# V2 on four column tiles, W1 behind W2, W0 on another queue: the start of a feature-interaction kernel, reordered

## The chip, the cores and the metric

The kernel runs on one core of one Trainium2 chip. The metric is device time in microseconds, the median over runs; less is better. The core has a matmul engine (TensorE, PE in the profile, its weight loads listed apart as PEld), a vector engine (DVE), a scalar engine (ACT), GpSimd (POOL) and SyncE (SP). PE writes to PSUM banks alone; DVE and ACT copy from there. ACT, POOL and SP each issue DMA transfers from a queue of their own; the 16 DMA engines of the core carry them all.

## The reference

`x` is 1024 x 39 x 64 (batch, field, embedding). Three layers of the same form follow one another; their sums over the embedding are weighted by `fc_w` and added.

```python
def _cin_layer(Xk, X0, W, b):
    O = W.shape[0]
    Hk, Fdim = (Xk.shape[1], X0.shape[1])
    Wr = W.reshape(O, Hk, Fdim)
    return jnp.einsum('bhe,bfe,ohf->boe', Xk, X0, Wr) + b[None, :, None]
X0 = sparse_embedding
Xk = X0
outs = []
for W, b in ((W0, b0), (W1, b1), (W2, b2)):
    Xk = _cin_layer(Xk, X0, W, b)
    outs.append(Xk.sum(axis=-1))
cin_output = jnp.concatenate(outs, axis=-1)
return cin_output @ fc_w.T + fc_b
```

W0 is 64 x 1521 (39 x 39 pairs of fields), W1 and W2 are 64 x 2496 (64 x 39). All is float32.

## The kernel before

**What it computes with.** The last two layers only feed one number per sample, so the kernel folds their weights: W2 and `fc_w` give `v2`, a 64 x 40 table (V2; its last column is the second third of `fc_w`); W1 and `v2` give T, for each pair of fields a column of 64. W0 turned and T lie side by side in `both`: W0's part in partitions 0 to 63, T's in 64 to 127. A symmetric pair of fields is then one row of weights (`pairs`), turned by PE into `wa`. The main work is a product of two fields' values for each pair (DVE, `product`, L210), multiplied on PE by `wa` into `po` (`multiply`, L502).

**Blocks.** The batch is 32 blocks of 32 samples (2048 columns). Each block has six chunks of 128 pairs; two blocks share a chunk of pairs left over (`join`, L522 and L533). The operands of the products are gathers: rows of a table in device memory (`xd`, three tables for two blocks each, every one with two rows of ones) picked by index lists that DVE computes at the start (`lists`, L313 to L374). `gather_rows` (L170) runs on POOL. For block 0 the tiles 0 to 3 are gathered in two halves from `xh`, two half blocks that are loaded straight from `x` (L244); tile 4 and everything later comes from `xd`, and `xd[0]` is copied from `xh` by SyncE (L383).

**The order of the start.** Every engine does its instructions in the order in which the program lists them.

- SyncE's queue: `fcrow` (L240), the first half `xh[0]` (L244), and later the two copies `xd[0]` from `xh` (L383).
- ACT's queue: W2 (L241), W0 in two parts (L250), W1 in two halves (L255), `xh[1]` (L244); then a first copy that brings in ACT's table (L259).
- POOL: constants, then the rows of ones for the three tables (L344), the biases and `fc_b` (L348 to L351, five small transfers), then the gathers: tiles 0 to 3 of the first half, the load of block 1, tiles 0 to 3 of the second half, tile 4 and so on.
- DVE: the lists, with the identity `unit` (L318) and `fc2` (L319) among them. `fc2` holds the last third of `fc_w`, twice, in two columns of zeros: column 0 for even rows, column 32 for odd rows, since W2 lies in 128 partitions, two for each output.
- PE: filler matmuls (`spin`, L271) whose results nobody reads; the `fcrow2` matmul that turns a row of `fc_w` (L310); fillers; V2's four matmuls (L393) into two banks `pv`; four more turned rows of `fc_w` (`turn_row`, L354); 20 transposes of W0 (L407) into two banks `pw`; then T's 39 matmuls (L439) into four banks, of which the last two are `pv`; three fillers; the first turn of `pairs` (L486), one filler, the first products (L502). A float32 matmul shows as two passes in the profile, a transpose as one.
- Between them DVE turns V2 by two block transposes (L413) and DVE and ACT copy it into `v2` (L418 to L420); both copy W0 (L435) and T (L450) into `both`, then build `pairs` (L466 to L470).

Transfers signal semaphores. Those of SP's and ACT's queues go round eight semaphores, POOL's round eight others; one that takes a semaphore again waits for the landing of the earlier transfer that has it.

Of the kernel before, what the change touches and what calls it, by code (L numbers as in the profile page):

```python
# [54 lines left out]
F32 = mybir.dt.float32  # L55
I32 = mybir.dt.int32
AF = mybir.ActivationFunctionType
ALU = mybir.AluOpType
# [3 lines left out]
FH = F * H  # L62
FT = F + 1
# [80 lines left out]
def cin_kernel(ctx: ExitStack, tc: tile.TileContext, x, w0t, b0, w1, b1, w2, b2, fc_w, fc_b, out):  # L144
# [71 lines left out]
    with prep as prep:  # L216
# [5 lines left out]
        fc2 = prep.tile([128, H], F32, name="fc2")  # L222
# [20 lines left out]
        def load_half(k, engine):  # L243
            engine.dma_start(  # L244
                xh[k].rearrange("f (b e) -> b f e", e=E), x[k * SB : (k + 1) * SB]
            )

        load_half(0, nc.sync)
        for s, n in enumerate((NW, F - NW)):
            nc.scalar.dma_start(  # L250
                w0s[H * s : H * s + F, 0 : n * H], w0v[:, s * NW * H : (s * NW + n) * H]
            )
        for s in range(2):
            part = slice(s * FH // 2, (s + 1) * FH // 2)
            nc.scalar.dma_start(w1s[:, part], w1[:, part])  # L255
# [6 lines left out]
        pv = [bank("pv") for _ in range(2)]  # L262
        pt = [bank("pt") for _ in range(2)] + pv
# [48 lines left out]
        )  # L312
        nc.vector.tensor_copy(row, place)  # L313
# [4 lines left out]
        nc.vector.tensor_scalar(unit, apart, 0, None, ALU.is_equal)  # L318
        nc.vector.tensor_scalar(fc2[:, 0::32], mask, small[:, 0:1], None, ALU.mult)  # L319
# [14 lines left out]
        nc.vector.tensor_scalar(lists[:, NT : 2 * NT], fields_of, float(FT), None, ALU.add)  # L334

# [7 lines left out]
        for k in range(NTAB):  # L343
            nc.gpsimd.dma_start(xd[k][F::FT].rearrange("r (p c) -> p r c", c=128), ones)  # L344


        for k, t in enumerate((b1, b2)):
            nc.gpsimd.dma_start(bias[:, k : k + 1], t.rearrange("(h o) -> h o", o=1))  # L348
        for h in (0, H):
            nc.gpsimd.dma_start(b0s[h : h + H], b0.rearrange("(h o) -> h o", o=1))  # L350
        nc.gpsimd.dma_start(fcb, fc_b.rearrange("(p o) -> p o", o=1))  # L351

        def turn_row(dst, k):
            nc.tensor.matmul(dst, fcrow[:, k * H : k * H + H], one, start=True, stop=True)  # L354

        spin(2)
# [31 lines left out]
        blocks = prep.tile([128, 2, 320], F32, name="blocks")  # L388
        w2v = w2s.rearrange("p (h f) -> p h f", f=F)
        for k in range(2):  # L390
            for u in range(2):
                f0 = u * 19 + k * 10
                nc.tensor.matmul(  # L393
                    pv[k][H * u : H * u + H, 0:320],
                    fc2,
                    w2v[:, :, f0 : f0 + 10],
                    start=True,
                    stop=True,
                )

        for k in range(3):
            turn_row(small[0:H, k + 1 : k + 2], k)
        turn_row(small[H:128, 4:5], 0)
        for s in range(2):
            for k in range(NW // 2):
                n = min(128, (F - NW * s) * H - k * 128)
                nc.tensor.transpose(  # L407
                    pw[s][0:n, k * FT : k * FT + F],
                    w0s[H * s : H * s + F, k * 128 : k * 128 + n],
                    unit[H * s : H * s + F, H * s : H * s + F],  # L410
                )
        for k in range(2):
            nc.vector.transpose(  # L413
                blocks[:, k].rearrange("p (f h) -> p f h", h=32),
                pv[k][:, 0:320].rearrange("p (h f) -> p f h", f=10),
            )
        column = blocks.rearrange("h k (f j) -> h (k f) j", j=32)[:, :, 0]
        nc.scalar.copy(v2[:, F:FT], small[0:H, 2:3])  # L418
        nc.vector.tensor_copy(v2[:, 0:20], column[0:H])
        nc.scalar.copy(v2[:, 20:F], column[H:128, 1:20])  # L420
# [8 lines left out]
        copies = (nc.vector.tensor_copy, nc.scalar.copy)  # L429

        for k, (a, n) in enumerate(((0, NW), (NW, F - NW))):
            for t in range(2):
                m = (n + 1 - t) // 2
                src = pw[k][H * t : H * t + H, 0 : m * FT].rearrange("h (a b) -> h a b", b=FT)
                copies[k](bothv[0:H, a + t : a + t + 2 * m - 1 : 2, 0:F], src[:, :, 0:F])  # L435
        w1v = w1s.rearrange("o (h f) -> o f h", f=F)
        for a in range(F):
            q, g, t = a // (2 * NQ), a // 2 % NQ, a % 2
            nc.tensor.matmul(  # L439
                pt[q][H * t : H * t + H, g * FT : g * FT + FT],  # L440
                w1v[:, a],
                v2,
                start=True,
                stop=True,
            )
        for q in range(4):
            for t in range(2):
                a = 2 * NQ * q + t
                m = len(range(a, min(F, 2 * NQ * (q + 1)), 2))
                copies[t](  # L450
                    bothv[H:128, a : a + 2 * m - 1 : 2],
                    pt[q][H * t : H * t + H, 0 : m * FT].rearrange("h (a b) -> h a b", b=FT),
                )
        spin(3)
# [268 lines left out]
```

## Time and profile before

| what | us |
|---|---|
| median of four runs | 741.48 |
| the four runs | 739.51 to 744.95 |
| the profiled execution | 738.22 |
| its span, first to last instruction | 736.4 |
| PE busy | 727.6 (99%) |
| DVE busy | 638.2 (87%) |
| ACT busy | 165.0 (22%) |
| POOL busy | 388.6 (53%) |
| V2's matmuls, from | 5.89 |
| W0's transposes, from | 7.63 |
| T's matmuls, from | 11.09 |
| first gather, from | 11.67 |
| first product matmul (L502), from | 21.54 |

All places are counted from the span's start. Busy shares are means over the whole span, so they hide the start, which lasts some 20 us of 736. A line of a timeline gives start, length, engine, line, operation, out<-in, the count, and in brackets the idle time before it with what ended it. "Issue" is time in which an engine waited for nothing that the profile shows.

### The profile page before, as it was taken

The page shows a single profiled execution, that of the slowest core. Times are in us where ns is not written, and L with a number is a line of the kernel's source. Part 1 is how long each engine was busy: PE and PEld are TensorE (multiplying, and loading weights), DVE is VectorE, ACT ScalarE, POOL GpSimd, SP SyncE. Part 2 cuts the span into 40 slices and gives each one's busy share as a digit, 9 for nine tenths or more (in the row PEclk, how much of TensorE's full clock was granted, in tenths as well). Part 3 has the DMA queues.
Part 4 walks back from the last instruction along what each step waited for, and adds up shares of the span by engine and source line. Part 5 has one row for each costly group of instructions (what it writes and reads, how often), then busy time and mean ns, then how long its engine had stood idle before and what let it go on. Part 6 is the DMA issues. An engine that isn't in the chain of part 4 may idle for free.

```text
span 736.4 us, 6511 instructions
## 1 busy us (share of the span) xinstructions
PE 727.6 (99%) x2456; PEld 319.6 (43%) x2456; DVE 638.2 (87%) x516; ACT 165.0 (22%) x238; POOL 388.6 (53%) x256
## 2 busy tenths in 40 slices
PE   7999999999999999999999999999999999999998
PEld 5444444444444444444444444444444444444443
DVE  4899999888899888899888899888899888899885
ACT  2232122221212222122221212222122221212222
POOL 6848864457545365554457545365554457545300
PEclk8899999999999999999999999999999999999999
DMA  7889997877676796757877676795767876566700
GB/s 201 296 334 354 337 394 296 335 283 273 239 277 253 291 347 237 270 238 276 330 277 277 238 278 255 288 356 220 267 251 271 335 284 252 213 259 247 285 1 1
DMA packets 63656, 197.25 MB, mean 268 GB/s; under 512 B 37684, under 2 KB 37733, under 8 KB 43656
## 3 DMA queue, kind: packets, MB, share of 16 engines
q0 software_dynamic: 29040, 186.22, 65.5%
q1 hardware_dynamic: 33534, 8.79, 5.2%
q10 hardware_dynamic: 1050, 1.83, 1.0%
q8 instruction: 19, 0.31, 0.2%
q14 instruction: 13, 0.11, 0.0%
HBM read 196.76 MB, written 10.60 MB: 282 GB/s over the span
## 4 chain that ended last, share of the span: by engine, by line
PE 97%; DMA 1%; DVE 1%; ACTq 0%; issue 0%; ACT 0%
PE po L502 90%; PE po L522 4%; PE po L533 2%; DMA w1s<-in_w 1%; PE idle L271 1%; PE pv L439 0%; PE pt L439 0%; DVE p L210 0%; PE tr L486 0%; ACTq L250 0%; DVE g L552 0%; DVE sums L574 0%; ACT z L550 0%; ACTq L255 0%; ACTq L241 0%
## 5 line engine op out<-in xcount | busy, mean ns | idle before, releaser
L502 PE MATMUL po<-p,wa 128*128 128x512 f32 x1536 | 665.2, 593 | 0.6 <-DVE p L210 0.6
L210 DVE TENSOR_TENSOR p<-r 128x2048 f32<-128x2048 f32 (+2 forms) x198 | 434.3, 2225 | 74.4 <-PE po L502 71.0
L170 POOL DMA_INDIRECT r<-xd,lists x156 | 307.6, 1972 | 282.9 <-issue 269.3
L502 PEld LDWEIGHTS po<-p,wa 128*128 128x128 f32 x1536 | 290.2, 190 | 371.3 <-issue 351.5
L550 ACT ACTIVATE z<-po,fc0s 64x512 f32<-64x512 f32 x128 | 87.4, 683 | 381.5 <-PE po L533 218.6
L552 DVE SCALAR_TENSOR_TENSOR g<-po,b0s,z 64x512 f32<-64x512 f32 x128 | 95.9, 749 | 9.3 <-ACT z L550 5.3
L545 ACT COPY g<-r 39x1024 f32<-39x1024 f32 x64 | 66.7, 1043 | 155.5 <-DVE sums L563 122.1
L563 DVE TENSOR_REDUCE sums<-g 103x16 f32<-103x1024 f32 x62 | 75.6, 1220 | 2.1
L170 POOL DMA_INDIRECT v<-xd,lists x16 | 29.3, 1829 | 4.9 <-issue 4.9
L170 POOL DMA_INDIRECT u<-xd,lists x16 | 29.1, 1819 | 4.9 <-issue 4.9
L522 PE MATMUL po<-p,wa 32*64 32x512 f32 x512 | 31.6, 600 | 0.0
L212 DVE TENSOR_TENSOR p<-u,v 128x1024 f32<-128x1024 f32 x16 | 19.5, 1217 | 0.0
L522 PEld LDWEIGHTS po<-p,wa 32*64 32x64 f32 x512 | 9.4, 131 | 20.2 <-issue 20.2
L533 PE MATMUL po<-u,wa 32*64 32x512 f32 x256 | 17.0, 587 | 0.0
L170 POOL DMA_INDIRECT r<-xh,lists x8 | 10.5, 1317 | 6.1 <-issue 6.1
L533 PEld LDWEIGHTS po<-u,wa 32*64 32x64 f32 x256 | 5.7, 132 | 8.0 <-issue 8.0
L271 PE MATMUL idle<-const-float32-1.0 128*128 128x256 f32 x16 | 8.0, 658 | 0.8 <-PEq L710 0.8
L469 DVE TENSOR_TENSOR pairs<-both 128x2 f32<-128x2 f32 (+27 forms) x59 | 6.0, 172 | 0.4 <-ACT both L450 0.4
L450 DVE COPY both<-pt 64x200 f32<-64x200 f32 x2 | 0.7, 358 | 6.0 <-PE pt L439 3.4
L487 ACT COPY wa<-tr 128x128 f32<-128x128 f32 x8 | 2.1, 266 | 15.5 <-PE tr L486 15.5
L271 PEld LDWEIGHTS idle<-const-float32-1.0 128*128 128x128 f32 x16 | 4.7, 327 | 1.7 <-issue 0.9
L164 POOL DMA_DIRECT2D xd<-in_x x5 | 5.3, 1069 | 0.0
(92 smaller groups left out, 55.8 us busy)
## 6 DMA issues: line engine op xcount, KB each, us to landing
xd<-in_x SPq DMA_DIRECT2D x26, 312.0 KB
r<-xd,lists POOLq DMA_INDIRECT x156
xd<-in_x POOLq DMA_DIRECT2D x5, 312.0 KB
w2s<-in_w ACTq DMA_DIRECT2D x1, 624.0 KB
w1s<-in_w ACTq DMA_DIRECT2D x2, 312.0 KB
xd<-xh SPq DMA_DIRECT2D x2, 156.0 KB
u<-xd,lists POOLq DMA_INDIRECT x16
v<-xd,lists POOLq DMA_INDIRECT x16
```

What stands on the lines that cost most here:

```text
L170: nc.gpsimd.indirect_dma_start(dst, None, table, bass.IndirectOffsetOnAxis(ap=lists[:, k : k + 1], axis=0))
L210: nc.vector.tensor_tensor(p[:, cols], r[:, i, cols], r[:, k, cols], ALU.mult)
L212: nc.vector.tensor_tensor(p[:, 0:SUB], ut[n // 2 % 2], vt[n // 2 % 2], ALU.mult)
L271: nc.tensor.matmul(idle[:, 0:cols], nc.const_aps.tensor(1.0, (128, 128), F32), nc.const_aps.tensor(1.0, (128, cols), F32), start=True, sto ...
L469: nc.vector.tensor_tensor(out, diagonal(a, b, sa, sb), diagonal(b, a, sb, sa), ALU.add)
L502: nc.tensor.matmul(po[n][m], wa[:, c, side : side + 2 * H], p[:, bass.ts(m, MM)], start=n % 2 == 0 and c == 0, stop=n % 2 == 1 and c == NP ...
L522: nc.tensor.matmul(dst[half * H : half * H + H], wa[rows, NPAIR, at : at + H], p[rows, bass.ts(side, MM)], start=t >= 2, stop=t < 2 and ha ...
L533: nc.tensor.matmul(dst[half : half + H], wa[rows, NPAIR + 1, H : 2 * H], ut[n // 2 % 2][rows, bass.ts(side, MM)], start=False, stop=t < 2,)
L545: nc.scalar.copy(gt[H : H + F], rt[n % 2][0:F, 0, bass.ts(m, SUB)])
L550: nc.scalar.activation(z[one], po[n][m][other], AF.Identity, bias=fc0s[other])
L552: return lambda: nc.vector.scalar_tensor_tensor(g[n][m // 2][0:H, at], po[n][m][one], b0s[one], z[one], ALU.add, ALU.mult)
L563: nc.vector.tensor_reduce(sums[:, b_at : b_at + SB], g[n][m // 2].rearrange("p (b e) -> p b e", e=E), AX.X, ALU.add,)
```

## The change

- **V2.** `fc2` is 32 columns wide with its two filled columns next to each other. V2's four matmuls go to four tiles of 32 columns of the array, each for ten fields (from fields 0, 10, 20 and 29, so field 29 is computed twice), and write one bank. One block transpose replaces two, and eight copies of 32 partitions, four on DVE and four on ACT, replace two.
- **Queues.** ACT's queue holds W2, W1's halves, `xh[1]`. SyncE's holds `fcrow`, `xh[0]`, the rows of ones, W0's two parts, the biases and `fc_b`, and the copies of L383. POOL issues no small transfers.
- **PE's order.** The turned rows of `fc_w` come right behind the `fcrow2` matmul, with two fillers behind them (one of 256 columns, one of 128) and two more like them behind V2's matmuls. W0's transposes stand between T's matmuls of fields 0 to 19 and of 20 to 38.
- **DVE's order.** `fc2` and `unit` are computed behind the field lists. W0's copies into `both` stand between T's second and third pair of copies.
- **Banks.** V2 has one bank; T has three of its own and V2's.

```diff
-        fc2 = prep.tile([128, H], F32, name="fc2")
+        fc2 = prep.tile([128, 32], F32, name="fc2")
...
         load_half(0, nc.sync)
+        for s in range(2):
+            half = slice(s * FH // 2, (s + 1) * FH // 2)
+            nc.scalar.dma_start(w1s[:, half], w1[:, half])
+        for k in range(NTAB):
+            nc.sync.dma_start(xd[k][F::FT].rearrange("r (p c) -> p r c", c=128), ones)
         for s, n in enumerate((NW, F - NW)):
-            nc.scalar.dma_start(
+            nc.sync.dma_start(
                 w0s[H * s : H * s + F, 0 : n * H], w0v[:, s * NW * H : (s * NW + n) * H]
             )
-        for s in range(2):
-            part = slice(s * FH // 2, (s + 1) * FH // 2)
-            nc.scalar.dma_start(w1s[:, part], w1[:, part])
         load_half(1, nc.scalar)
...
-        pv = [bank("pv") for _ in range(2)]
-        pt = [bank("pt") for _ in range(2)] + pv
+        pv = bank("pv")
+        pt = [bank("pt") for _ in range(3)] + [pv]
...
+        for at, k, h in ((1, 0, 0), (2, 1, 0), (3, 2, 0), (4, 0, H)):
+            nc.tensor.matmul(
+                small[h : h + H, at : at + 1],
+                fcrow[:, k * H : k * H + H],
+                one,
+                start=True,
+                stop=True,
+            )
+        spin()
+        spin(1, MM // 4)
...
-        nc.vector.tensor_scalar(unit, apart, 0, None, ALU.is_equal)
-        nc.vector.tensor_scalar(fc2[:, 0::32], mask, small[:, 0:1], None, ALU.mult)
...
+        nc.vector.tensor_scalar(fc2[:, 0:2], mask, small[:, 0:1], None, ALU.mult)
+        nc.vector.tensor_scalar(unit, apart, 0, None, ALU.is_equal)
...
-        for k in range(NTAB):
-            nc.gpsimd.dma_start(xd[k][F::FT].rearrange("r (p c) -> p r c", c=128), ones)
...
         for k, t in enumerate((b1, b2)):
-            nc.gpsimd.dma_start(bias[:, k : k + 1], t.rearrange("(h o) -> h o", o=1))
+            nc.sync.dma_start(bias[:, k : k + 1], t.rearrange("(h o) -> h o", o=1))
         for h in (0, H):
-            nc.gpsimd.dma_start(b0s[h : h + H], b0.rearrange("(h o) -> h o", o=1))
-        nc.gpsimd.dma_start(fcb, fc_b.rearrange("(p o) -> p o", o=1))
+            nc.sync.dma_start(b0s[h : h + H], b0.rearrange("(h o) -> h o", o=1))
+        nc.sync.dma_start(fcb, fc_b.rearrange("(p o) -> p o", o=1))
...
-        spin(2)
...
+        blocks = prep.tile([128, 10, 32], F32, name="blocks")
         w2v = w2s.rearrange("p (h f) -> p h f", f=F)
+        quarters = (0, 10, 20, 29)
+        for u, f0 in enumerate(quarters):
+            nc.tensor.matmul(
+                pv[32 * u : 32 * u + 32, 0:320],
+                fc2,
+                w2v[:, :, f0 : f0 + 10],
+                start=True,
+                stop=True,
+            )
+        nc.vector.transpose(
+            blocks.rearrange("p f h -> p (f h)").rearrange("p (f h) -> p f h", h=32),
+            pv[:, 0:320].rearrange("p (h f) -> p f h", f=10),
+        )
+        spin()
+        spin(1, MM // 4)
+        nc.scalar.copy(v2[:, F:FT], small[0:H, 2:3])
+        for u, f0 in enumerate(quarters):
+            for s in range(2):
+                lo = u == 3
+                copies[s](
+                    v2[32 * s : 32 * s + 32, f0 + lo : f0 + 10],
+                    blocks[32 * u : 32 * u + 32, lo:, s],
                 )
...
+        turn_t(range(NW))
+        for k in range(NW // 2):
+            for s in range(2):
+                n = min(128, (F - NW * s) * H - k * 128)
+                nc.tensor.transpose(
+                    pw[s][0:n, k * FT : k * FT + F],
+                    w0s[H * s : H * s + F, k * 128 : k * 128 + n],
+                    unit[H * s : H * s + F, H * s : H * s + F],
+                )
+        turn_t(range(NW, F))
+        copy_t(0)
+        copy_t(1)
+        for k, (a, n) in enumerate(((0, NW), (NW, F - NW))):
+            for t in range(2):
+                m = (n + 1 - t) // 2
+                src = pw[k][H * t : H * t + H, 0 : m * FT].rearrange("h (a b) -> h a b", b=FT)
+                copies[k](bothv[0:H, a + t : a + t + 2 * m - 1 : 2, 0:F], src[:, :, 0:F])
+        copy_t(2)
+        copy_t(3)
         spin(3)
```

`turn_t(fields)` holds T's matmuls for the fields given, `copy_t(q)` the two copies of one of T's four banks; both hold the code that stood in line before.

## The prediction

> **What bounds the kernel now.** The page's chain of waits comes first. PE holds 97% of it and the 128x512 product matmul on L502 holds 90%, so from the moment that stream runs, only PE's own pace counts.
>
> ```profile
> PE 97%; DMA 1%; DVE 1%; ACTq 0%; issue 0%; ACT 0%
> PE po L502 90%; PE po L522 4%; PE po L533 2%; DMA w1s<-in_w 1%; PE idle L271 1%; PE pv L439 0%; PE pt L439 0%; DVE p L210 0%; PE tr L486 0%; ACTq L250 0%; DVE g L552 0%; DVE sums L574 0%; ACT z L550 0%; ACTq L255 0%; ACTq L241 0%
> ```
>
> The diff touches no line of the stream, so I asked for the chain of the first 36 us in order of time (start, length, what).
>
> ```profile
> 2.79 8.16 DMA w1s<-in_w
> 10.96 0.14 issue
> 11.09 2.65 PE pt L439 x40
> 13.74 2.03 PE pv L439 x28
> ...
> 16.43 0.92 issue
> 17.35 0.47 PE pv L439 x3
> 17.82 2.86 PE idle L271 x6
> ...
> 21.75 1.12 PE po L502 x2
> ```
>
> Read it as a sum: W1 lands at 10.96; T, 78 passes on L439, takes 6.73 us to 17.82; the filler matmuls of L271 and a transpose take 3.93 us; then the stream begins at 21.75. T's passes start 63 ns apart, so 78 need 4.9 us: 1.8 us of T is standstill, the 0.92 above and shorter gaps from 15.0 on. No semaphore ends them; PE's only 16 KB instruction transfer of this time runs from 15.29 for 0.95 us, so I take them for code loading.
>
> The table of windows, cut where the granted clock changes, shows the clock (after the span: busy us and count of PE, PEld, DVE, ACT, POOL; then clock, DMA share, GB/s).
>
> ```profile
> 8.48:11.89 3.41, 1.14 (x20) 1.05 (x18) 1.11 (x2) 0.93 (x2) 0.22 (x1) 1.00 0.55 126
> 11.89:15.31 3.42, 3.42 (x58) 3.42 (x58) 0.36 (x1) 0.32 (x1) 2.73 (x3) 0.50 0.48 144
> 18.72:22.14 3.42, 3.42 (x9) 2.42 (x8) 3.42 (x18) 0.75 (x6) 2.81 (x3) 0.50 1.01 378
> ```
>
> Half clock holds from 11.89 to 22.14. T doesn't feel it: its passes start 62 to 63 ns apart before 11.89 as after. A 128x256 filler pass does (0.427 us against 0.216 for half of a 0.431 us stream pass), and so does the stream's beginning.
>
> Last, what the gathers wait for (L170 on POOL's queue; L383 on SP's), and the only long stop of PE behind the stream's start.
>
> ```profile
> L170 POOLq EVENT_SEMAPHORE  x4: 17/43/3908, 7.0 to 22.6; - x4
> ...
> L383 SPq EVENT_SEMAPHORE  x2: 17/17/17, 7.0 to 11.8; - x2
> ...
> 34.39 2.29 DVE L210 TENSOR_TENSOR p<-r 128x2048 f32<-128x2048 f32 x1 [1.92 <-PE po L502]
> ...
> 36.83 1.10 PE L502 MATMUL po<-p,wa 128*128 128x512 f32 x2 [0.65 <-DVE p L210]
> ```
>
> POOL's first gather stands 3.9 us, from 6.97. Its operands say on what: semaphore 108, which the first small table row (L344, POOL's queue) signals too, landing at 10.84. POOL's eight DMA semaphores go round, and the eight small transfers used them first. The chain puts the DVE wait at 34.39 on PE; the semaphore records show tile 4's gather landing at 34.27, and that fits better.
>
> **The change, part by part.** Times are of the profiled execution, 738.22 us (span 736.4 and 1.8 around it); the median shown is 741.48, 3.26 above. I move the median by the sum.
>
> *V2.* Two block transposes (0.475 and 0.511 us) become one. Two copies become eight of 32 partitions: four on DVE, four on ACT, at most 0.17 and 0.22 us each by L419 and L420, so up to 0.5 and 0.66 more. W2 lands at 5.75. On DVE, fc2's and unit's instructions move behind the lists; the 0.65 us wait for the fcrow2 matmul goes, so the last list (end 7.37) ends near 6.8. The eight matmul passes, 1.38 us before, end by 7.2. The transpose ends near 7.7, V2 is ready near 8.4, as now (8.44). That costs nothing while W1 lands later, which covers it; if W1 lands at 7.9, T waits some 0.5 for V2.
>
> *W1 ahead of W0.* The best rows are W1's own landings. Three of the 16 landings of its second half come at 7.89, 8.58 and 8.66, the others at 9.43 to 10.96. W0's 39 rows go over 13 engines (13 landings of its first part, 5.40 to 6.46), so I read the three as the engines with no W0 row ahead of W1. Bounds: 7.89 and 10.96. I take 8.6. That supposes that W0 doesn't run beside W1 on SP's queue, and the trace speaks for it: SP's and ACT's DMAs share eight semaphores (100, 103 to 107, 116, 117), and L383 signals 100 and 103 again, waiting for them. Eighteen DMAs now go round them before L383 is done, so from the ninth each waits for an older landing. SP holds fcrow, xh's first half, three table rows, W0 twice, five small ones and L383's two copies in order; W0's second part should wait for W2 (5.75) or xh (6.94), so it issues at 5.8 to 7.5. T starts at 8.7 in place of 11.09: **-2.4**.
>
> The Trainium skill speaks against this: "DMA: Bandwidth & Descriptors", section "Issuing engines are not separate DMA queues", says that DMAs of all issuers run on the same engines and interleave, so another queue puts nothing behind W1. By that rule alone W0's bytes run among W1's, W1 lands near 10.5 and the term is -0.5.
>
> *W0 between T's halves.* PE runs in order. The 20 transposes on L407 took 1.19 us, then under T's wait for W1; now nothing covers them: **+1.2**. Their copies (1.13 us DVE, 0.94 ACT, L435) lie under T's second half, 2.4 us of PE; without that cover they would add 1.1. If W0 lands after T's first half (8.7 + 2.55 = 11.25), PE stands. The nearest row is L383's first copy: 39 rows on SP's queue, issued 7.02, landed 12.34. Bounds 0 and 1.1; I take **+0.25**, landing 11.5.
>
> *Code loading.* The passes up to T's end rise from 124 to 128, so the fetch falls in T's second half: **0**, bounds -1.8 (something else waits meanwhile) and 0.5. T then ends at 16.87 instead of 17.82.
>
> *Fillers and clock.* The last three fillers stay. Those moved ahead (1.5 in place of two before V2's matmuls, 1.5 more behind them) lie under the waits for W2 and W1. Clock changes lie at 5.07, 11.89 and 22.14, so on a 3.41 us grid, and the window 11.89 to 15.31 shows PE busy throughout without full clock following. So I expect half clock to 22.14 again, and a stream that starts 0.95 earlier gains half of it: **+0.47**. Bounds: 0, and -0.85 more if the clock rises early; past that the stream catches up with DVE's products (the second half of step 2's is ready 0.85 ahead of its use).
>
> Against this row stands the skill's page "TensorE: Matmul & The Clock Gate", Part 1: about 3.4 us of sustained matmuls bring full clock. By that rule T would have raised it by 15.31, and the fillers behind T would cost 1.3 us less.
>
> *Gathers.* With POOL's small DMAs gone, its semaphores are fresh and only xh (6.94) holds the first gather: 7.0 instead of 11.67. The first product's second operand landed at 19.0 for a use at 19.14; it comes some 4 us earlier, so it doesn't hold an earlier stream. Tile 4's gather (25.73, landed 34.27) should come near 21, land near 30; the 0.65 us stop goes: **-0.65**, bounds 0 and -1.1 (with the 0.47 us PE stop at 42.05). It reads L383's copies, now behind five small DMAs on SP, perhaps held until xh's second half lands (11.46); landing near 17, they have 3 us in hand. The biases' later landing meets first uses past 47 us.
>
> Sum: -2.4 + 1.2 + 0.25 = -0.95 for T's end; +0.47; -0.65: **-1.13 us**. 738.22 would become 737.1; the median 741.48 becomes 740.35, **740.3**.
>
> **Rivals.**
> *A, the forecast:* 740.3. Its own range: with no wait for W0, nothing lost to the clock and -1.1 from the gathers, 739.2; with W1 at 9.4, the first of the other landings, 741.1. Chance 0.50.
> *C, both standstills go:* code arrives under another wait (-1.8) and the clock rises early (0.47 saved, 0.85 more). 740.35 - 1.8 - 1.32 = 737.2. For it: T's continuous work now begins inside one grid window. Against: the busy window without full clock. 0.20.
> *D, the order buys nothing:* W0 and the earlier gathers run beside W1, which lands at 10.5. T ends at 10.6 + 2.55 + 1.2 + 2.4 + 1.8 = 18.55, +0.7; with -0.65 about 741.6. For it: gathers issued at 7.0 bring packets from 8.3 (1.3 us after issue, as at 13.0 now). Against: three landings by 8.66. 0.15.
> *B, W0 comes late:* T's second half is locked behind it on PE. T's end is landing + 5.4, so with the gathers' -0.65 the kernel is slower from a landing at 13.1. The gathers issued from 11.67 to 15.53 took 4.6 to 6.0 us under full DMA, tile 4's 8.5. Issued at 7.0, W0 lands at 11.6 to 15.5; at 15 the sum is +2.6 - 0.65, or 743.4. Against it: L383's copy landed within 5.3. 0.15.
>
> **How the numbers follow.** About 0.5% (3.7 us) is what a measurement of this kernel can tell from no change: below 737.8 or above 745.2. A and D lie inside. C lies at the lower edge, and with what the terms leave open most of it counts as faster, 0.18 in all; B's tail gives slower 0.07; the rest, 0.75, is within. The range, 737.2 to 743.2, takes in C's and nearly B's centre.
>
> **What would show it.** W1's wait on L439 ending near 8.6; T starting before 9; the transposes of W0 directly behind 40 passes (a gap there is B); gaps late in T (gone: C); the first gather near 7.0; the stop at 36.8 gone; half clock until the grid point next after T. I am wrong if W1 lands after 10, W0 after 12, or V2 holds T.

## The result, and the profile after

The changed kernel took 742.16 us (median of 52 runs, 739.12 to 748.81), the kernel before 740.13 beside it (78 runs): a ratio of **1.0025**, interval 1.0012 to 1.0037, some 1.9 us slower (2.0 by the two medians). The forecast was 1.13 us faster; the change is within the 0.5% named there, with the other sign. The profiled execution of the changed kernel took 742.38 us, with a span of 740.6 (before: 738.22 and 736.4).

The chain of waits of the changed kernel for the first 36 us, in order of time (start, length, what):

```profile
1.12 8.15 DMA xh<-in_x
...
9.28 2.88 DMA w0s<-in_w0t
...
12.34 1.24 PE pw L452 x19
...
18.45 0.36 DVE both L443
18.81 3.27 another core or an unknown queue
22.08 0.02 issue
22.10 0.36 DVE both L443
```

W1 no longer stands in it. W0 does, held by `xh[0]`, whose semaphore W0's second part takes again. The step to look at is the 3.27 us that the view gives to "another core or an unknown queue". There is no other core. PE's own timeline and DVE's show what it is (start, length, line, operation, count, idle time before with what ended it). First PE:

```profile
16.06 0.22 PE L431 MATMUL pt<-v,w1s 64*64 64x40 f32 x1 [0.97 <-issue]
...
16.21 1.29 PE L431 MATMUL pv<-v,w1s 64*64 64x40 f32 x17
17.43 2.93 PE L273 MATMUL idle<-const-float32-1.0 128*128 128x256 f32 x6
23.62 0.45 PE L499 MATMUL tr<-unit,pairs 128*128 128x128 f32 x1 [3.26 <-DVE pairs L482]
```

then DVE's copies of W0 (L464) and T (L443):

```profile
16.18 1.14 DVE L464 COPY both<-pw 64x390 f32<-64x390 f32 x2 [2.63 <-remote]
18.45 0.36 DVE L443 COPY both<-pt 64x200 f32<-64x200 f32 x1 [1.14 <-PE pv L431]
22.10 0.36 DVE L443 COPY both<-pv 64x200 f32<-64x200 f32 x1 [3.29 <-remote]
```

T's last pass is recorded as ended at 17.50 (the profile models the ends of matmuls), and the copy that needs it starts at 22.10. When work is done, its engine raises a semaphore, and the one that waits goes on; below this is called the signal. PE's signal for T's last pass came at 22.08, **4.6 us behind the recorded end**; W0's was 2.6 us behind its own. The copies, the sums of L482 and PE's next transpose follow from there.

The windows, cut where the granted clock changes (span, then busy us and count of PE, PEld, DVE, ACT, POOL; clock, DMA share, GB/s):

```profile
18.79:22.20 3.41, 1.57 (x4) 0.67 (x2) 0.12 (x2) 0.32 (x1) 2.65 (x3) 0.50 1.03 396
22.20:25.62 3.42, 2.00 (x4) 1.11 (x5) 3.07 (x18) 1.19 (x7) 2.13 (x3) 0.50 1.03 420
25.62:29.04 3.42, 3.42 (x6) 1.45 (x5) 3.42 (x18) 0.38 (x2) 3.12 (x2) 0.50 1.03 413
```

PE is half idle from 18.79 to 25.62, and half clock lasts to 29.04 instead of 22.14. So the difference of the two profiles adds up: the stream starts at 24.71 instead of 21.54, 3.17 later; it runs 4.33 us at half clock instead of 0.60, which costs (4.33 - 0.60) / 2 = 1.87 more; the stop of 0.65 near tile 4 is gone. That makes 4.4; the spans differ by 4.2.

### The profile page after: what moved, and what is told of

The parts are those of the page before. It is cut to its first block, busy times and chain, and to the rows that moved or that the text cites. A ratio compares the mean times of both kernels' runs of the same rounds, so it can differ in the third digit from the quotient of the medians.

```text
span 740.6 us, 6521 instructions
## 1 busy us (share of the span) xinstructions
PE 731.0 (99%) x2460; PEld 321.5 (43%) x2460; DVE 637.8 (86%) x518; ACT 165.5 (22%) x241; POOL 387.5 (52%) x248
## 3 DMA queue, kind: packets, MB, share of 16 engines
q1 hardware_dynamic: 34104, 9.23, 5.4%
## 4 chain that ended last, share of the span: by engine, by line
PE 97%; DMA 1%; another core or an unknown queue 0%; DVE 0%; issue 0%; ACT 0%; SPq 0%
PE po L515 90%; PE po L535 4%; PE po L546 2%; DMA xh<-in_x 1%; DMA w0s<-in_w0t 0%; PE pv L431 0%; PE pt L431 0%; PE tr L499 0%; PE pw L452 0%; PE idle L273 0%; DVE g L565 0%; DVE both L443 0%; DVE sums L587 0%; ACT z L563 0%
## 5 line engine op out<-in xcount | busy, mean ns | idle before, releaser
L170 POOL DMA_INDIRECT r<-xd,lists x156 | 313.7, 2011 | 284.7 <-issue 273.2
L170 POOL DMA_INDIRECT r<-xh,lists x8 | 7.8, 973 | 8.9 <-DMA w0s<-in_w0t 6.7
L273 PE MATMUL idle<-const-float32-1.0 128*128 128x256 f32 (+1 forms) x20 | 9.3, 622 | 0.8 <-PEq L723 0.8
L482 DVE TENSOR_TENSOR pairs<-both 128x2 f32<-128x2 f32 (+27 forms) x59 | 6.0, 172 | 0.4 <-issue 0.4
L431 PE MATMUL pt<-v,w1s 64*64 64x40 f32 x60 | 4.5, 297 | 1.8 <-issue 1.0
L499 PE MATMUL tr<-unit,pairs 128*128 128x128 f32 x8 | 2.6, 320 | 3.7 <-DVE pairs L482 3.3
L443 DVE COPY both<-pt 64x200 f32<-64x200 f32 x3 | 1.1, 359 | 5.8 <-PE pt L431 4.7
```

The costliest lines, as they stand in the source:

```text
L170: nc.gpsimd.indirect_dma_start(dst, None, table, bass.IndirectOffsetOnAxis(ap=lists[:, k : k + 1], axis=0))
L273: nc.tensor.matmul(idle[:, 0:cols], nc.const_aps.tensor(1.0, (128, 128), F32), nc.const_aps.tensor(1.0, (128, cols), F32), start=True, sto ...
L482: nc.vector.tensor_tensor(out, diagonal(a, b, sa, sb), diagonal(b, a, sb, sa), ALU.add)
```

## The experiments

Two things could be meant by those late signals: something that the change does, or something that comes to both kernels from outside (the kernel before has signals 2.2 and 2.5 us behind T's second and third quarter). The chip of the first result is not recorded; the second to seventh are numbered here in the order in which they came. Letters such as P and L are theories, each set out in the expectation of its run.

### Variants of the changed kernel (second chip)

**The load of block 1 on SyncE's queue** (e1). In both profiles a standstill of PE lies over this DMA's instruction on POOL.

```diff
-                load(1, nc.gpsimd)
+                load(1, nc.sync)
```

> The changed kernel with one DMA moved: the load of x's second block (load(1), called at L385) issues from SyncE's queue in place of GpSimd's. In both profiled executions a standstill of PE lies over the span of that DMA's instruction on POOL (changed kernel: PE stands 15.09 to 16.06, the instruction runs 15.03 to 16.09; kernel before: 16.43 to 17.35 and 16.48 to 17.56). Theory P (POOL's descriptor work for this DMA stops PE): no standstill of PE near 15.1 to 16.1, T's second half ends about 1.0 us earlier (near 16.5), and the late signal of T's last quarter (22.08) comes earlier by 1 us or more; time about 1.0 us under the changed kernel's. Theory L (PE works T slower than its records show while the clock is half): the standstill is the queue between PE's sequencer and the array running full, so it stays near its place whatever POOL does; T's end within 0.3 us; POOL's later gathers come 1.1 us earlier; time within 0.7 us of the changed kernel's.

**The small transfers back on POOL's queue** (e2); `b0s` and `fcb` go the same way.

```diff
-            nc.sync.dma_start(xd[k][F::FT].rearrange("r (p c) -> p r c", c=128), ones)
...
+            nc.gpsimd.dma_start(xd[k][F::FT].rearrange("r (p c) -> p r c", c=128), ones)
...
-            nc.sync.dma_start(bias[:, k : k + 1], t.rearrange("(h o) -> h o", o=1))
+            nc.gpsimd.dma_start(bias[:, k : k + 1], t.rearrange("(h o) -> h o", o=1))
```

> The changed kernel with the eight small transfers (three rows of ones, both biases, b0 twice, fc's bias) back on GpSimd's queue; everything else as changed. Theory Q (landings held by shared semaphores on SyncE's queue cost the time): xh's first half lands near 7 instead of 9.27, W0 near 10 to 11 instead of 12.16, so PE's 0.32 us stand before W0's turn goes; the first gather goes back to about 11.7. Time 1 to 2 us under the changed kernel's. Theory G (the earlier gathers' traffic slows T and its signals): T's last signal comes nearer to its recorded end (under 2 us behind in place of 4.6), the stop near tile 4 returns (0.65 us); time about 1 us under. Theory L (half clock and W0's turn inside T): PE's order is the same, so T's last signal stays 3 us or more behind the recorded end, half clock until 25 or later; time within 0.7 us of the changed kernel's.

**W0's turn behind T** (e3), its copies into `both` behind T's as well.

```diff
         turn_t(range(NW))
+        turn_t(range(NW, F))
         for k in range(NW // 2):
...
-        turn_t(range(NW, F))
```

> The changed kernel with the 20 transposes of W0 behind all of T instead of between its halves, and W0's copies behind T's. Theory Q (W0's late landing, 12.16, holds T's second half): T ends 1.2 + 0.3 us earlier, W0's turn lies behind it; W0's copies (about 1 us on DVE and ACT) now come last, so the first pairs come no earlier than before: time within 0.7 us of the changed kernel's. Theory L (the array falls behind its records by a fixed pace at half clock): the last PE signal that the copies wait for is as late as now (22.1 within 0.5 us), whichever of T and W0 is last. Theory S (the turn of W0 between T's halves is itself what delays PE's signals, a change between transposes and passes): T's last signal comes 2 us or more earlier.

**T's second half twice** (e4).

```diff
         turn_t(range(NW, F))
+        turn_t(range(NW, F))
```

> The changed kernel with T's second half (38 passes) run twice over, the second time over the same results: 38 more passes for PE, nothing else. Theory R (the records are right: 62 ns a pass, and the late signal is a delay on its way): T's recorded end moves by 2.4 us, the last signal by about as much or less, and the time by 2.4 us or less. Theory L (the array works a pass of T in 110 to 150 ns at half clock, and the queue hides it): the second 38 passes show 110 ns or more each in the records, as the queue is full by then, or T's last signal moves by 4 us or more; the time is 4 to 5.5 us over the changed kernel's.

| run | time, us | ratio to the kernel before (737.94) | T's last pass and its signal | stream from | later stops of PE over 0.5 us |
|---|---|---|---|---|---|
| e1 load on SyncE | 740.38 | 1.0026 (1.0010 to 1.0041) | 15.35, 15.36 | 19.05 | 3.67 at 34.6 |
| e2 small on POOL | 738.23 | 1.0001 (0.9989 to 1.0013) | 16.99, 17.00 | 20.41 | none |
| e3 W0 behind T | 736.62 | 0.9982 (0.9969 to 0.9995) | 14.16, by 14.20 | 19.09 | 2.12 at 45.4 |
| e4 half of T twice | 737.29 | 0.9986 (0.9967 to 1.0005) | 17.96, 17.98 | 21.68 | none |

None of the four has late signals or a standstill in T, so no theory of what brings them about could be tried as it was meant. P (POOL's work for the load stops PE) is not borne out: the load's instruction stays on POOL in e2, e3 and e4, and PE does not stop under it. L (at half clock PE works slower than its records show) is refuted for half clock as such: in e4 76 passes run 66 ns apart ahead of full clock (22.79), and the last is signalled 0.02 us behind its end. The kernel with 2.4 us *more* of PE's work has a lower ratio than the changed kernel in its first result. All four are variants; e5 and e6 below are the changed kernel itself, and their signals are on time too, so the late signals are not a fixed part of this program.

What e1 lost has its own cause: SyncE's copies into the table came behind the load, tile 4's gather started at 27.9, and PE stood for it at 34.6.

e2 also shows what the landing of W1 hung on. Its chain, and e4's (W0 held on SyncE's queue as in the changed kernel):

```profile
1.79 8.64 DMA w1s<-in_w
```

```profile
1.79 7.19 DMA w1s<-in_w
```

With the rows of ones off SyncE's queue, W0's parts issue at 1.86 and 2.71, run beside W1 and W1 lands at 10.43; held by shared semaphores (e4), they issue at 5.99 and 8.46, and W1 lands at 8.97. So it was the held semaphore that put W0 behind W1, and not the other queue. The Trainium skill's page "DMA: Bandwidth & Descriptors", section "Issuing engines are not separate DMA queues", says that transfers of all issuers interleave on the same engines. e2 agrees: without the hold it measured 10.43 where the prediction had 10.5 by that rule.

### The two kernels again, on other chips

> The changed kernel once more, for a second profile of it beside runs of the kernel before on this chip. In its first profile PE's signals came up to 4.6 us behind the recorded end of T, PE stood 3.26 us ahead of the first transpose of weights, the clock was half until 29.04 and the stream began at 24.71. Theory H (that is how this program runs: the order of PE's work and the late landing of W0 bring it about): the second profile shows the late signals again, the stream begins at 23 or later; ratio to the kernel before 1.0025 again. Theory V (the late signals come and go from one execution to the next, in both kernels): this profile shows none, as the four kernels derived from the changed one showed none; T ends near 15.4 and the stream begins near 19, held by the second gather's landing as in the kernel with W0 behind T; the ratio is again near 1.0025, since it is a median over executions of both kinds.

> The changed kernel, a third profile. Theory H: late signals (2 us or more behind T's recorded end) here too. Theory V: with a chance of its own, independent of the second profile; a profile without them has the stream begin at 18.8 to 20.

> The kernel before, a second profile. In its first one T's second and third quarters were signalled 2.2 and 2.5 us behind their recorded ends and PE stood 0.92 us in T. Theory V: these may be absent here; then T, begun near 11.1, ends near 16.1 instead of 17.82, and the stream begins near 19.8 instead of 21.54. Theory H: they come again and the stream begins at 21.5 within 0.3 us.

> The changed kernel a third time, in the hope of another chip. So far: on the chip of the first result it took 1.0025 of the kernel before's time, and its profile there had late PE signals (T's last 4.6 us behind its recorded end); on the chip of the second profile it took 0.9982, with no signal later than 0.1 us. Theory V, now sharper (the late signals belong to the chip, or to what goes on around it, and cost the changed kernel more than the one before): a profile without late signals goes with a ratio of 0.996 to 1.000, one with them with 1.001 to 1.004, and the kernel before is near 738 in the first case and near 740 in the second. Theory M (the ratio has nothing to do with the late signals): a ratio over 1.001 without late signals, or under 0.999 with them.

> The changed kernel on whichever chip this lands. Theory V: with PE's signals on time the ratio lies at 0.996 to 1.000 and the stream begins at 18.5 to 19.7; with late signals it lies at 1.001 to 1.004 and the stream begins at 23 or later. Theory M: any other pairing.

> The changed kernel on a further chip. Theory V: with PE's signals on time the ratio lies at 0.996 to 1.000 and the stream begins at 18.5 to 19.8; with late signals the ratio lies at 1.001 to 1.004 and the stream begins at 23 or later. Theory M: any other pairing.

> The kernel before, one profile on the same chip. With signals on time its T takes 5.0 us (from about 11.1 to 16.1), the first product starts at 18.8 to 19.5 with the second gather's landing as its last wait, and the stream begins at 19.8 to 20.4. With late signals: T ends later than 17 and the stream begins at 21 or later.

| chip | kernel before, us | changed, us | ratio | T in the profile of the changed kernel, from, to, signalled | stream from |
|---|---|---|---|---|---|
| first result | 740.13 | 742.16 | 1.0025 (1.0012 to 1.0037) | 9.23, 17.50, 22.08 | 24.71 |
| third (e5, e6) | 738.09 | 736.62 | 0.9982 (0.9963 to 1.0001) | 9.08, 15.51, 15.52 | 18.82, 19.12 |
| fourth (e9) | 738.06 | 736.48 | 0.9987 (0.9974 to 1.0000) | 8.87, 15.86, 15.87 | 19.57 |
| fifth (e12) | 738.05 | 737.43 | 0.9995 (0.9978 to 1.0012) | 8.95, 16.00, 16.01 | 19.71 |
| sixth (e13) | 738.08 | 736.58 | 0.9969 (0.9952 to 0.9986) | 9.18, 15.94, 15.96 | 19.34 |

As first put (ahead of e5), theory V had late signals come and go from one execution to the next and the ratio stay near 1.0025; e5's 0.9982 speaks against that. As put ahead of e9 (they go with the chip, or with what goes on around it), all five rows agree: where PE's signals are on time the changed kernel is faster, by 1.2 us on the mean of the four ratios (0.9983; three of the four intervals reach 1 by themselves), and the kernel before takes 738. With late signals, on the one chip that has both kernels, both are slower, and the changed one loses more. A second profile of the kernel before (e7, third chip) is without late signals as well. Its PE timeline:

```profile
11.07 2.64 PE L439 MATMUL pt<-v,w1s 64*64 64x40 f32 x40 [2.45 <-DMA w1s<-in_w]
13.49 2.62 PE L439 MATMUL pv<-v,w1s 64*64 64x40 f32 x38
```

and its DVE timeline:

```profile
16.86 0.65 DVE L469 TENSOR_TENSOR pairs<-both 128x4 f32<-128x4 f32 x6 [0.35 <-ACT both L450]
19.32 0.69 DVE L210 TENSOR_TENSOR p<-r 128x512 f32<-128x512 f32 x1 [1.81 <-DMA r<-xh,lists]
```

T takes 5.0 us, not 6.73. The 16 KB instruction transfer is there too (15.72, for 1.09 us) and PE does not stop for it. And with T on time, **the first product waits 1.81 us for the second gather** and is ready at 20.01, level with the fillers behind T, which end at 20.03; in e15 PE waits 0.51 us for that product. So T alone does not bound the start of the kernel before. In the changed kernel of the fourth chip the product waits too:

```profile
18.26 0.69 DVE L210 TENSOR_TENSOR p<-r 128x512 f32<-128x512 f32 x1 [1.00 <-DMA r<-xh,lists]
```

but it is ready at 18.95, ahead of its use, and the chain of waits there runs from T through the fillers to the stream:

```profile
14.66 1.19 PE pv L431 x18
15.86 2.85 PE idle L273 x6
18.71 0.21 PE tr L499
18.93 0.85 PE idle L273 x2
19.78 1.05 PE po L515 x2
```

In all five profiles of the changed kernel with signals on time PE goes from T to the stream without such a wait, and the product is ready 0.1 to 0.7 us ahead of the first pass that needs it. In the changed kernel's profiles on these chips T ends at 15.4 to 16.0 and the second gather lands at 17.6 to 18.4; in the two of the kernel before (e7, e15) T ends at 16.1 and 15.6, the gather lands at 19.2 and 18.4, and the stream starts at 20.16 and 19.35. So the start is some 0.4 us earlier on the mean (19.31 against 19.76). The rest lies in later stops: 1.93 and 3.77 us in the two profiles before, 2.28 and 2.25 in e5 and e6, none over 0.5 in e9, e12 and e13 (e5 has one more, 0.94). Seven profiles are too few to part the 1.2 us between the two, and both of the kernel before, at 740.71 and 741.73, are among its longer executions (median 738.1).

### The small transfers alone, and W0's turn again

**The kernel before with the eight small transfers on SyncE's queue** (e8, e10, e18), nothing else:

```diff
-            nc.gpsimd.dma_start(xd[k][F::FT].rearrange("r (p c) -> p r c", c=128), ones)
+            nc.sync.dma_start(xd[k][F::FT].rearrange("r (p c) -> p r c", c=128), ones)
...
-            nc.gpsimd.dma_start(bias[:, k : k + 1], t.rearrange("(h o) -> h o", o=1))
+            nc.sync.dma_start(bias[:, k : k + 1], t.rearrange("(h o) -> h o", o=1))
```

> The kernel before with one part of the change alone: its eight small transfers issue on SyncE's queue instead of GpSimd's. By the reading of the shared semaphores, the first gather then waits for xh's first half alone and starts near 7.5 to 9.5 instead of 11.67; T starts as before (10.9 to 11.1) or later. Theory Q (held landings): SyncE's copies into the table (L383) land later than 17, the stream begins no later than before, and the time is within 0.7 us of the kernel before's. Theory G (the earlier gathers take the DMA engines from W1 and from what T waits for): W1 lands at 11.3 or later and T starts as much later; the time is 0.5 to 2 us over the kernel before's. If the gathers bound the beginning, and nothing is held: 0.7 to 1.5 us faster.

> The kernel before with the small transfers on SyncE's queue, again, beside the changed kernel on one chip. If the whole gain of the change comes from the gathers' earlier start, and W1's earlier landing, the turn of W0 between T's halves and V2 on four column tiles buy nothing on top of it (T then ends before the second gather's data are there): this kernel takes no more than the changed one on any chip, 0.996 to 0.999 of the kernel before's time; on a chip with late signals it stays under 1.000, since W0's turn and its copies lie ahead of them as in the kernel before. If the other parts do help, it is slower than the changed kernel by 0.5 us or more on a chip without late signals.

> The kernel before with the small transfers on SyncE's queue, a third time. Theory T (on some chips PE's passes of T come late or in bursts while the gathers' data flow, so gathers that start earlier cost more there): where T runs its 5.0 us, ratio 0.997 to 0.999 and a stream from 19.5 or so; where T takes longer than 7 us, ratio 1.001 to 1.005. Against it: a ratio under 0.999 with a T of more than 7 us (the loss of the two kernels with the load moved then came from that load), or over 1.001 with a T of 5 us.

It took 735.87, 736.06 and 735.84 us: ratios 0.9973 (0.9959 to 0.9987), 0.9981 (0.9968 to 0.9994) and 0.9978 (0.9962 to 0.9994). Beside the changed kernel on the same chip it was 0.75, 0.42 and 1.59 us under it (third, fourth and fifth chip), each time less than their spread. e2, with all of the change but this, took 1.0001. So on chips with signals on time this part alone brings the gain, and the other parts add nothing that shows. The chain of e8's first 36 us:

```profile
10.87 2.63 PE pt L439 x40
13.50 2.39 PE pv L439 x38
15.89 2.86 PE idle L271 x6
18.75 0.21 PE tr L486
```

Its first gather starts at 7.71, as `xh[0]` lands at 6.84, and the second lands at 14.8; in the changed kernel `xh[0]` lands at 8.3 to 9.27 and the second gather at 17.6 to 18.4. With the gathers out of the way, T and the fillers bound the start. But the stream begins at 19.35 to 19.61 in e8, e10 and e18, no earlier than in the changed kernel: the gain is not at the start. None of the three has a stop of PE over 1 us behind it.

**W0's turn behind T, beside the changed kernel** (e14, sixth chip): 736.11 against 736.58.

> The changed kernel with W0's turn behind T, beside the changed kernel on one chip. With signals on time: within 1 us of the changed kernel, since the first product waits for the second gather (landing near 17.8) in both, and T's end does not. With late signals: if they act through the turn between T's halves, 1.5 us or more under the changed kernel; if not, within 1 us of it.

Ratio 0.9970 (0.9952 to 0.9989) against 0.9969: its place makes no difference that shows where signals are on time. With late signals this was not tried.

**One filler behind T instead of three, on e8** (e11, fifth chip):

```diff
-        spin(3)
+        spin(1)
```

> The kernel before with the small transfers on SyncE's queue and one filler matmul in place of three behind T (two passes of PE instead of six). In that kernel with three, PE's passes end at 18.75 to 18.98, while the first weights' sums are ready at 17.3 to 17.5: the fillers hold the first transpose by about 1.3 us. Theory F (the fillers are in the way, the clock comes anyway): the transpose starts near 17.5, the stream near 18.4, full clock not later than 21.7; 0.8 to 1.2 us under the kernel with three fillers (736.06 where the kernel before takes 738.06), ratio about 0.996. Theory K (the fillers bring the clock): full clock comes one grid step of 3.41 us later, which takes back 1.7 us: ratio 0.998 to 1.000. Theory D (the DMA engines bound the first 55 us): the stream begins earlier, but PE stops as much longer near 45, where block 1's tiles land: ratio 0.997 to 0.999.

736.69 us, 0.9981 (0.9965 to 0.9996), beside 0.9978 for three fillers on the same chip (e18). The stream began at 19.03 instead of 19.35, full clock came at 22.68 instead of 19.59, and PE stopped for 1.01 at 45.8 and 1.25 at 61.4: both K (the fillers bring the clock) and D (PE stops longer later), and nothing gained.

### Where the later stops come from, and a chip with bursts

Beside e1 (see above) and e17, seven profiles have a stop of PE of 1 us or more that a gather ends, six near 45 (e3, e5, e6, e7, e11, e14; two of them another of 1.2 near 61) and one at 35 (e15). These stops go with most of the spread: on the five chips with signals on time the eight profiled executions that have one took 738.87 to 741.73 us, the eight without 734.95 to 737.69, whichever the kernel. All seven show the same on POOL: one gather's instruction takes 6.36 us (6.37 in e11) where the others of the first 40 us take 0.93 to 2.9. In the six it is the first small table's, and block 1's tiles come late; in e15 it is tile 4's. POOL's timeline of e7, and then its PE timeline:

```profile
25.92 6.36 POOL L170 DMA_INDIRECT u<-xd,lists  x1 [0.30 <-DVE pairs L469]
32.58 0.94 POOL L170 DMA_INDIRECT v<-xd,lists  x1 [0.30 <-issue]
```

```profile
48.45 2.28 PE L502 MATMUL po<-p,wa 128*128 128x512 f32 x3 [1.93 <-DVE p L210]
```

In e9, e12 and e13 the same instruction takes 3.95 us, in e4, e8, e10 and e18 the long one (6.35 to 6.57) is the second small table's, one place later, and none of them stops there. In e3, e6, e7 and e15 the stop is followed by 3.41 us of half clock, which costs 1.7 more.

To see whether the amount that POOL has issued sets this, the load of block 1 went to SyncE's queue behind the two copies, once on e8 (e16) and once on the changed kernel (e17):

```diff
-            if not k:
-                load(1, nc.gpsimd)
...
             nc.sync.dma_start(xd[0][0:F, cols], xh[k])
+        load(1, nc.sync)
```

> The kernel before with the small transfers on SyncE's queue and, as well, the load of x's second block (1248 elements) issued from SyncE behind the two copies into the table instead of from GpSimd between the gathers. Theory W (POOL's queue is full when it has issued so much more than has landed; then one instruction stands 6.36 us): with that load gone from it, the stand comes at least one gather later or not at all, no PE stop over 1 us near 35 to 47, and the time is 0.5 to 1.5 us under the kernel with the small transfers moved alone, ratio 0.995 to 0.9975. Theory Z (the stand has to do with time, not with amounts): it comes at the same gather within one place, and the time stays within 0.7 us of that kernel's, ratio 0.997 to 0.999.

> The changed kernel with the same move of the load. Theory W: the stand of 6.36 us comes later or not at all, the time is 0.5 to 1.5 us under the changed kernel's, ratio 0.9955 to 0.998. Theory Z: ratio 0.997 to 0.9995. Against both: SyncE's copies land only near 20 in the changed kernel, and the load lands behind them; if it comes later than block 1's first gather wants it (near 31), PE stops and the kernel is slower than the changed one.

On the seventh chip they took 743.39 and 743.78 us, 1.0043 (1.0014 to 1.0072) and 1.0054 (1.0032 to 1.0075). But the kernel before took 741.49 there (19 runs, 737.92 to 752.06), and T was far from its 5.0 us, so their times tell nothing of W (POOL's queue is full when it has issued so much more than has landed) or Z (amounts do not matter). The place of the long instruction does: in e16 it is the second small table's again, 6.36 us (6.35 in e8), and in e17 the first one's, 6.78, though the load is gone from POOL and POOL had stood for 8.9 and 9.2 us just ahead of the small tables. That speaks against W. They also show something else. PE's timeline of e16:

```profile
12.92 0.82 PE L438 MATMUL pv<-v,w1s 64*64 64x40 f32 x7
...
15.16 0.45 PE L438 MATMUL pv<-v,w1s 64*64 64x40 f32 x3 [0.70 <-issue]
16.60 0.22 PE L438 MATMUL pv<-v,w1s 64*64 64x40 f32 x1 [0.99 <-issue]
17.33 0.32 PE L438 MATMUL pv<-v,w1s 64*64 64x40 f32 x1 [0.51 <-issue]
...
20.87 0.46 PE L438 MATMUL pv<-v,w1s 64*64 64x40 f32 x3 [0.49 <-issue]
21.58 0.22 PE L438 MATMUL pv<-v,w1s 64*64 64x40 f32 x1 [0.25 <-issue]
22.29 1.29 PE L438 MATMUL pv<-v,w1s 64*64 64x40 f32 x17 [0.49 <-issue]
```

From 13.7 on, T's passes come in ones and threes, from 15.16 on at distances of 0.71 to 0.73 us or twice that, and nothing that the profile shows ends the pauses. T lasts to 23.59. Its first quarter, recorded by 11.9, is signalled at 15.88, and the second, recorded by 13.1, at 22.37. So late signals and the bursts come together. e17 has both as well: T from 8.57 to 23.44, bursts from 14.2 on.

## Why the prediction was wrong

The forecast was 1.13 us faster; the runs of the first result say 1.9 slower, the four other chips 1.2 faster. The mean of the latter fits by luck: the reasons given are not what brought it.

**The step that failed in the first result** is *code loading*: standstills put down to an instruction fetch, priced at "0, bounds -1.8 (something else waits meanwhile) and 0.5", with T's end at 16.87. T's last signal came at 22.08, 5.2 us past that, where the upper bound allowed 0.5. The 1.8 us of standstill in T before belong to that execution or its chip, and not to the program: e7 and e15 have the instruction transfer and no standstill. Nor does the transfer fit: before, it had ended at 16.24 when the longest standstill began (16.43 to 17.35), and in the changed kernel it began at 16.56, when the standstill (15.09 to 16.06) was over. The semaphore times of the first profile had pointed to it (signals 2.2 and 2.5 us behind the recorded passes), and they were not laid beside the records of PE. What the runs showed in its place is PE late by up to 4.6 us; why it is late stays open.

**Fillers and clock**, +0.47 with half clock to 22.14: measured to 29.04, as PE stood idle for 3.26 us behind T. The step had taken the 3.93 us from T's end to the stream (3.72 by the timeline's 21.54) as fixed; it was 7.2 by the records and 2.6 from the last signal. The step also took the grid of clock changes from one profile; its place differs from profile to profile (half clock begins at 11.97, 11.39, 11.52 and 11.88 in the four of the changed kernel that show it). On the other chips, where the clock's rows begin ahead of T (e5, e12, e13), full clock came at 18.22, 21.75 and 18.71. And in the forecast's own range the 741.1 for W1 at 9.4 keeps the clock's +0.47, though T's end would gain only 0.15 there; with half of that, some 0.1, it is 740.8.

**Gathers.** The first was forecast for 7.0 and came at 10.13 (9.2 to 10.1 elsewhere). The step took `xh[0]`'s landing, 6.94, over from the kernel before without asking what would now run beside it: 9.27. What delays it is not shown. It is not W1's place alone, since e2 has W1 there and `xh[0]` landed at 7.35, nor the rows of ones behind it on SyncE's queue alone (6.84 in e8). The second gather was to land some 4 us earlier than 19.0; with signals on time it lands at 17.6 to 18.4, and DVE waits some 1 us for it. That it "doesn't hold an earlier stream" came true, but narrowly: the first product is ready 0.1 to 0.7 us ahead of its use, so a T that ended earlier still, where the sum lay, would have gained no more than that.

**What was right.** V2's parts lie under the wait for W1 and cost nothing (V2 ready at 8.34, forecast 8.4). T started at 9.23 for 8.7, W1's landing 9.09 for 8.6; the shared semaphores held W0 as worked out (its second part waited for `xh[0]`, though to 9.28 where 7.5 was the latest forecast). W0's turn took 1.25 us for 1.2, its wait 0.32 for 0.25, though W0 landed at 12.16 and not 11.5. The stop of 0.65 near tile 4 is gone in all profiles of the changed kernel. Rival C, both standstills gone, describes T on the on-time chips better than the forecast does: it ends at 15.4 to 16.0 (C: 15.1). Rivals D and B did not come about in any profile of the changed kernel: W1 landed by 9.1 and W0 held PE by at most 0.4 us.

**What stays open.** It is not settled what makes PE late on some chips, nor whether it is the chip or the time at which it ran. It is not the half clock alone (e5 and e7 have it during T and are on time), not the instruction transfer, not W0's place alone (the kernel before and e16 are late without it), not the load's instruction on POOL (in e16 and e17 SyncE issues the load, and T is late all the same). The bursts lie where the gathers' data flow (DMA share 0.85 to 1.06 from 12 to 24 in e16), and the kernels whose gathers start earlier are hit over more of T; this fits theories G and T (the gathers' traffic slows T), and was not isolated: e8 shows a share of 0.85 to 1.04 there without any bursts. The 6.36 us on POOL goes with the long stops; what sets its length and place is open too. The small transfers alone were not run on a chip with late signals, so that this version is faster is shown for chips with signals on time, and there against the kernel before.

## What to carry to other kernels

Lay the time at which an engine's semaphore rises beside the recorded end of its work: where they are apart, a standstill is no property of the program, and one profile is not enough to price what lies there. When a transfer takes another's place, ask what it now runs beside. When a first operand comes from a gather, find its landing before pricing the matmuls ahead of it: work that ends ahead of that landing buys nothing by ending earlier. Where executions of one kernel differ by more than the change is worth, find out what they differ by.

## What the hardware showed unexpectedly

- PE's signals up to 4.6 us behind recorded ends in the first profiles of both kernels, and more than that, with T's passes in bursts 0.72 us apart, on one of the six chips tried after them (which may be the same one); on the other five T takes 5.0 us, W0's turn apart.
- T's short passes do not feel the clock (66 ns apart in e4 while the fillers behind them take 0.43 us each); what slows them is something else.
- One gather's instruction of some 4 or 6.4 us on POOL in the first 40 us among others of 0.93 to 2.9, nearly always at tile 4's or one of the small tables' (e2 has none), with stops of PE of 1 to 3.8 us behind it in seven profiles.

T's short passes do not bring full clock, and the fillers do. The clock changes 3.41 us apart, or a multiple of that. In e15 PE is busy throughout two such windows; T's passes fill the first, and the fillers take 2.57 us of the second (rows as in the windows above):

```profile
11.23:14.64 3.41, 3.41 (x62) 3.41 (x60) 0.96 (x3) 0.64 (x2) 2.66 (x3) 0.50 0.52 189
14.64:18.05 3.41, 3.41 (x20) 2.84 (x19) 1.12 (x8) 0.87 (x3) 2.80 (x4) 0.50 0.89 258
18.05:21.46 3.41, 2.72 (x9) 1.20 (x8) 2.95 (x12) 1.02 (x7) 2.80 (x3) 1.00 1.00 349
```

Behind T, full clock follows the window in which the fillers take 2.57 us or more (e15, e5, e13, e1: 2.57, 2.78, 2.84, 3.40), and not one with 2.44 or less (e7, e12, e8: 2.38, 2.41, 2.44); these come one window later, e7 at 21.84, though PE was busy without a gap from 11.07 to 20.03. The Trainium skill's page "TensorE: Matmul & The Clock Gate", Part 1, has some 3.4 us of sustained matmuls bring full clock. The fillers agree with that (in e1 they run from 15.35 and full clock comes at 19.03), T's passes do not: 3.41 us of them left the clock at half in e15.
